# Residual additions of the mixer layers: from VectorE to an identity product on TensorE and bias reads on ScalarE

## The chip, the cores and the metric

The kernel runs on one core of one Trainium2 chip. The metric is the device time of the whole program in microseconds (us): the median over several runs. One execution was also taken with the hardware profiler, and all lines of a profile in this document come from such an execution.

## The reference, cut to what matters

The input is 16 sequences of 512 positions with 128 features, in fp32. Two blocks of the form x = x + s * silu(g) follow each other. In the first block, s comes from a four-layer "mixer" stack and g from a mixture of 8 experts; in the second block, s comes from windowed attention and g from a mixture of 32 experts with one shared expert. Both s and g read the normalised x. The change touches one thing alone, the layers of the first block's mixer stack:

```python
def _layer(x, p):
    ln1w, ln1b, aw, ab, pw, pb, ln2w, ln2b, fw, fb, mw, mb = p
    x = x + _attention(_layernorm(x, ln1w, ln1b), aw, ab, pw, pb)
    h = _layernorm(x, ln2w, ln2b)
    h = jax.nn.gelu(h @ fw + fb, approximate=False) @ mw + mb
    return x + h
for i in range(L):            # L = 4
    x = _layer(x, ...)
```

Here `_attention` is a projection to q, k and v, elementwise quaternion products of the three, a spectral filter over heads and head dimensions, and an output projection `pw` with bias `pb`. So each layer adds its input x twice to a product: once to the attention projection, once to the second MLP product, each time with a bias per feature.

## The kernel before, in words

Features lie on the 128 partitions and positions on the free axis. The program has two phases. The first, up to about 2,900 us, holds the mixer stack and both mixtures of experts. The second, from there to 4,108 us, is the windowed attention of the second block; the change does not touch it.

In the first phase four mixer streams p = 0 to 3 (`mixer_stream`) run side by side. Each takes the eight even or the eight odd sequences, one half of 256 positions each time, and takes every half through four layers (`mixer_layer`). There are 16 sequences x 2 halves x 4 layers = 128 mixer layers in all. Every stream has one PSUM bank of its own, `m0` to `m3`, with a single buffer: each product of a layer takes the bank over from the product before it, once that one has been read. The layer normalisation (`norm`) squares the sequence on ScalarE (line 185), takes the mean by one-column products (L189), adds eps on ScalarE (L198), raises to -0.5 on GpSimd (L200), spreads the result over the partitions by products with the identity (L203), and multiplies on VectorE (L213). The features have been rotated beforehand so that the mean sits in one component and drops out of the variance.

The residual sums are these two statements, one after the projection (`po`, L506) and one after the second MLP product (`pm`, L524):

```python
nc.vector.scalar_tensor_tensor(s1, in0=po, scalar=turned[:, l, 0:1], in1=s, op0=ALU.add, op1=ALU.add)
nc.vector.scalar_tensor_tensor(s2, in0=pm, scalar=turned[:, l, 1:2], in1=s1, op0=ALU.add, op1=ALU.add)
```

They are L508 and L526. Each is followed by a `yield`, and then by a norm of its result: s1 goes to the layer's second norm, s2 to the first norm of the next layer, or out of the stack after the fourth.

The experts share the four engines with the mixers. `loop0` takes one sequence through 8 experts of 256 hidden columns (products L299, L301, L305; Silu L303; multiplication L304), one expert at each of its steps; `loop1` takes one through 16 pairs of experts and the shared one (products L405, L407, L419; Silu L409; multiplications L410 and L418). `prep0` and `prep1` normalise and route. `loop1` of a sequence can start only when both of its mixer halves have written x (`written`), and the mixers of a sequence need what `prep0` and `loop0` leave in `given`.

The order of the work is set in two stages. First, Python generators write the program out: each turn advances every mixer stream by one `yield`, and feeds the experts by a rate, so that `due` steps come due:

```python
STEPS_M, STEPS_0, STEPS_1 = 41, 9, 18
pair = turn // STEPS_M
rate = ((STEPS_0 if pair < 7 else 0) + (STEPS_1 if pair else 0)) / (2 * STEPS_M)
```

41 is the number of yields that a mixer stream takes for one half sequence: ten in each of four layers and one at the end. Second, a scheduler puts the instructions of each engine in a fixed order when the program is built. It prefers those written out earlier, and mixer instructions count as 400 places earlier than they are (`AHEAD`). On the chip each engine then works through its own list in order.

Of the kernel before, what the change touches and what calls it, by code (L numbers as in the profile page):

```python
# [11 lines left out]
AF = mybir.ActivationFunctionType  # L12
ALU = mybir.AluOpType
# [7 lines left out]
L = 4  # L21
# [26 lines left out]
W_QKV, W_PROJ, W_FC, W_MP, W_END = 0, 3, 4, 8, 12  # L48
# [7 lines left out]
def recurrent_kernel(ctx: ExitStack, tc: tile.TileContext, a, out):  # L56
    nc = tc.nc
# [29 lines left out]
    ident = cst[:, C_ID : C_ID + P]  # L87
# [8 lines left out]
    filt = cst[:, C_G : C_G + S]  # L96
# [21 lines left out]
    turned = const.tile([P, L, 2], F32, name="turned")  # L118
# [54 lines left out]
            nc.vector.tensor_copy(w[:, first : first + n, :].rearrange("p j m -> p (j m)"), pt[:, : n * P])  # L173


    def norm(src, dst, sq, bank, name, xs=None, p="e"):


        if xs is not None:
            xc = bank(f"xc_{name}")  # L180
            nc.tensor.matmul(xc, lhsT=centre, rhs=src, start=True, stop=True)
            nc.scalar.activation(sq, xc, AF.Square)
            nc.scalar.copy(xs, xc)
        else:
            nc.scalar.activation(sq, src, AF.Square)
        pv = bank(f"pv_{name}")
        n = src.shape[-1] // P
        for k in range(n):
            nc.tensor.matmul(  # L189
                pv[:, k : k + 1],  # L190
                lhsT=sq[:, k * P : (k + 1) * P],
                rhs=mean_col if xs is not None else mean_col0,
                start=True,
                stop=True,
            )
        yield
        ve = small.tile([P, NBLK], F32, tag=f"ve{p}", name=f"ve_{name}", bufs=2)
        nc.scalar.activation(ve[:, :n], pv[:, :n], AF.Identity, bias=eps)  # L198
        rs = small.tile([P, NBLK], F32, tag=f"rs{p}", name=f"rs_{name}", bufs=2)
        nc.gpsimd.tensor_tensor(rs[:, :n], in0=ve[:, :n], in1=nhalf[:, :n], op=ALU.pow)  # L200
        bc = bank(f"bc_{name}")
        for k in range(n):
            nc.tensor.matmul(  # L203
                bc[:, k * P : (k + 1) * P],
                lhsT=rs[:, k : k + 1].to_broadcast([P, P]),
                rhs=ident,
                start=True,
                stop=True,
            )
        if xs is not None:  # L210
            nc.vector.tensor_mul(dst, bc[:, : n * P], xs)
        else:
            nc.vector.tensor_mul(dst[: P - 1], bc[: P - 1, : n * P], src[: P - 1])  # L213
        yield
# [209 lines left out]
        yield  # L424


    def mixer_layer(l, s, big, A, filt, last, bank, pool, name, p):


        first, last = last  # L430
        w = lw[l]


        qkv = big.rearrange("p (i c) t -> p i c t", c=4)

        sq, h, z = big[:, 1, :], normed[p], big[:, 0, :]
        yield from norm(s, h, sq, bank, f"{name}a", p=p)
        raw, steps, turns = qkv[:, :, 0, :], qkv[:, :, 1, :], qkv[:, :, 3, :]
        for at in (slice(0, 2), slice(2, 3)):
            pq = bank(f"pq{at.start}_{name}")[:, : (at.stop - at.start) * T]  # L440
            for i in range(at.start, at.stop):
                j = (i - at.start) * T
                nc.tensor.matmul(pq[:, j : j + T], lhsT=w[:, W_QKV + i, :], rhs=h, start=True, stop=True)
            pq = pq.rearrange("p (i t) -> p i t", t=T)
            nc.scalar.copy(raw[:, at], pq)

            nc.scalar.activation(turns[:, at], pq, AF.Identity, bias=quarter, scale=1.0 / (2.0 * math.pi))
        for i in range(3):

            nc.sync.dma_start(qkv[8:, i, 2, :], qkv[: P - 8, i, 0, :])  # L450
            nc.sync.dma_start(qkv[:8, i, 2, :], qkv[P - 8 :, i, 0, :])
        for i, n in ((0, 2), (2, 1)):
            at = slice(i, i + n)
            d = (raw[:, at, 1:T], raw[:, at, 0 : T - 1])
            nc.gpsimd.tensor_sub(steps[:, at, 1:T], *(d if i else d[::-1]))
            if not first:
                d = (raw[:, at, 0:1], last[:, at].unsqueeze(2))
                nc.gpsimd.tensor_sub(steps[:, at, 0:1], *(d if i else d[::-1]))
        if first:
            nc.gpsimd.memset(steps[:, :, 0:1], 0.0)  # L460
            nc.gpsimd.tensor_copy(last.unsqueeze(2), raw[:, :, T - 1 : T])
        yield

        n = A[:, 0:3, :]
        nc.vector.tensor_scalar_add(
            n.rearrange("p i (u t) -> p u i t", u=2), turns.rearrange("p i (u t) -> p u i t", u=2), MAGIC
        )
        nc.vector.scalar_tensor_tensor(turns, in0=n, scalar=-MAGIC, in1=turns, op0=ALU.add, op1=ALU.subtract)
        for at, scale in ((slice(0, 3, 2), -TWO_PI_BELOW), (slice(1, 2), TWO_PI_BELOW)):
            nc.scalar.activation(turns[:, at, :], turns[:, at, :], AF.Sin, scale=scale)  # L470
        yield
        q, k, vv = (qkv[:, i, :, :] for i in range(3))

        def rows(x, m):

            x = x.rearrange("p (b a) t -> p a b t", a=2)
            x = x[:, ::-1] if m & 1 else x
            return x[:, :, ::-1] if m & 2 else x


        for m in range(4):
            pr = pool.tile([P, 2, 2, T], F32, tag=f"pr{p}", name=f"pr_{name}{m}", bufs=1)
            nc.vector.tensor_mul(pr, rows(q, 0), rows(k, m))
            first, second = pr[:, 0], pr[:, 1]
            if m == 0:
                nc.vector.tensor_sub(first, first, second)
                nc.vector.tensor_sub(A[:, 0, :], first[:, 0, :], first[:, 1, :])
            elif m == 1:
                nc.vector.tensor_add(first, first, second)
                nc.vector.tensor_add(A[:, 1, :], first[:, 0, :], first[:, 1, :])  # L490
            elif m == 2:
                nc.vector.tensor_sub(first, second, first)
                nc.vector.tensor_add(A[:, 2, :], first[:, 0, :], first[:, 1, :])
            else:
                nc.vector.tensor_add(first, first, second)
                nc.vector.tensor_sub(A[:, 3, :], first[:, 0, :], first[:, 1, :])
        nc.vector.tensor_mul(A, A, vv)
        nc.vector.tensor_add(A[:, 0:2, :], A[:, 0:2, :], A[:, 2:4, :])
        yield

        py = bank(f"py_{name}")[:, :T]
        for i in range(2):
            nc.tensor.matmul(py, lhsT=dht, rhs=A[:, i, :], start=(i == 0), stop=(i == 1))
        nc.vector.tensor_mul(z, py, filt)
        po = bank(f"po_{name}")[:, :T]
        nc.tensor.matmul(po, lhsT=w[:, W_PROJ, :], rhs=z, start=True, stop=True)  # L506
        s1 = pool.tile([P, T], F32, tag=f"s{p}", name=f"s1_{name}", bufs=2)
        nc.vector.scalar_tensor_tensor(  # L508
            s1, in0=po, scalar=turned[:, l, 0:1], in1=s, op0=ALU.add, op1=ALU.add
        )  # L510
        yield
        yield from norm(s1, h, sq, bank, f"{name}b", p=p)
        hid = A
        for i in range(0, 4, 2):
            pf = bank(f"pf{i}_{name}")
            for j in range(2):
                nc.tensor.matmul(
                    pf[:, j * T : (j + 1) * T], lhsT=w[:, W_FC + i + j, :], rhs=h, start=True, stop=True
                )
            nc.scalar.activation(hid[:, i : i + 2, :], pf.rearrange("p (j t) -> p j t", t=T), AF.Gelu)  # L520
        yield
        pm = bank(f"pm_{name}")[:, :T]
        for j in range(4):
            nc.tensor.matmul(pm, lhsT=w[:, W_MP + j, :], rhs=hid[:, j, :], start=(j == 0), stop=(j == 3))  # L524
        s2 = pool.tile([P, T], F32, tag=f"s{p}", name=f"s2_{name}", bufs=2)
        nc.vector.scalar_tensor_tensor(  # L526
            s2, in0=pm, scalar=turned[:, l, 1:2], in1=s1, op0=ALU.add, op1=ALU.add
        )
        yield
        return s2  # L530

    def mixer_stream(seqs, half, pool, bank, p, given, written):

        at = slice(half * T, (half + 1) * T)
        for b in seqs:
            name = f"f{b}h{half}"
            while b not in given:
                yield
            z, _, last = given[b]
            s = z[:, at]  # L540
            for l in range(L):
                big = pool.tile([P, 12, T], F32, tag=f"big{p}", name=f"big_{name}l{l}")
                A = pool.tile([P, 4, T], F32, tag=f"A{p}", name=f"A_{name}l{l}")
                s = yield from mixer_layer(
                    l, s, big, A, filt[:, at], (half == 0, last[:, l, :]), bank, pool, f"{name}l{l}", p
                )
            while given[b][1] is None:
                yield
# [400 lines left out]
```

## Time and profile before

| | us |
|---|---|
| median of 3 runs | 4114.49 |
| lowest and highest | 4114.02, 4125.91 |
| the profiled execution | 4109.77 |
| its span, first to last instruction | 4108.0 |
| busy in the span: TensorE (PE) | 3861.7 |
| VectorE (DVE) | 3461.3 |
| ScalarE (ACT) | 2465.7 |
| GpSimd (POOL) | 1641.1 |

The profile names PE for TensorE's products and PEld for its weight loads, DVE for VectorE, ACT for ScalarE, POOL for GpSimd and SP for the engine that issues most of the transfers. A product of fp32 operands shows as two pairs of weight load and matmul, so the counts of PE are twice the number of calls. "Idle before" is the time in which an engine stood still just ahead of an instruction, and the releaser named after it is what ended that. The view by stretches of time gives each engine's busy time between two moments; the view of waits sums who waited for whom.

### The profile page before, as it was taken

The numbers are of one execution on the slowest core, as the hardware profiler recorded it, in microseconds if no ns is written. First come the engines' busy times: TensorE is split into PE (matmuls) and PEld (weight loads), VectorE is DVE, ScalarE is ACT, GpSimd is POOL, SyncE is SP. The second block draws the span as 40 slices with busy tenths as digits, with TensorE's granted clock in tenths as the row PEclk, the third lists the DMA queues.
The fourth block names the chain that finished last, engine by engine and source line by source line (L and its number), as shares of the span: only waits on it lengthen the run. The fifth ranks groups of instructions, "written<-read, shape, count | busy, mean of one in ns | idle before, by whom it ended". The sixth has DMA issues, their size and how long they took to land. (4 is left out here: it accounts for less than half of the span.)

```text
span 4108.0 us, 56711 instructions
## 1 busy us (share of the span) xinstructions
PE 3861.7 (94%) x16936; PEld 2329.9 (57%) x16936; DVE 3461.3 (84%) x8220; ACT 2465.7 (60%) x5543; POOL 1641.1 (40%) x1885
## 2 busy tenths in 40 slices
PE   8999999998999999999999998879999999999999
PEld 5555666665655656556566555544455555555555
DVE  5788999899889989989988999985677777777776
ACT  3555566655756556556655654633577777777776
POOL 1222322223222232222232223220577777777776
PEclk9999999999999999999999999989999999999999
DMA  3222333323332332442343232424100000000000
GB/s 116 80 82 85 97 90 114 113 73 109 122 91 87 112 112 80 120 120 78 104 122 95 77 114 84 123 66 134 59 11 19 14 19 14 11 19 14 19 4 6
DMA packets 205971, 308.95 MB, mean 75 GB/s; under 512 B 29664, under 2 KB 121952, under 8 KB 205536
## 3 DMA queue, kind: packets, MB, share of 16 engines
q1 hardware_dynamic: 205520, 304.28, 24.9%
q8 instruction: 135, 2.21, 0.2%
q14 instruction: 172, 1.41, 0.1%
q10 hardware_dynamic: 144, 1.05, 0.1%
HBM read 236.79 MB, written 18.09 MB: 62 GB/s over the span
## 5 line engine op out<-in xcount | busy, mean ns | idle before, releaser
L409 ACT ACTIVATE h_m<-pg_m 128x512 f32<-128x512 f32 x272 | 162.2, 596 | 280.5 <-PE pg_m L405 199.3
L405 PE MATMUL pg_m<-xn_m,w_m 128*128 128x512 f32 x544 | 289.3, 614 | 37.6 <-DMA w_m<-in_ew 25.8
L305 PE MATMUL acc_e<-h_e,w_e 128*128 128x512 f32 x512 | 273.8, 617 | 23.9 <-DVE h_e L304 23.6
L419 PE MATMUL acc_m<-h_m,w_m 128*128 128x512 f32 x544 | 284.6, 606 | 8.2 <-DVE h_m L418 8.1
L407 PE MATMUL pu_m<-xn_m,w_m 128*128 128x512 f32 x544 | 287.1, 610 | 5.6 <-DVE h_m L410 5.3
L299 PE MATMUL pg_e<-xn_e,w_e 128*128 128x512 f32 x512 | 268.7, 606 | 12.1 <-ACT h_e L303 10.6
L303 ACT ACTIVATE h_e<-pg_e 128x512 f32<-128x512 f32 x256 | 152.6, 596 | 202.7 <-PE acc_e L305 114.8
L301 PE MATMUL pu_e<-xg_e,w_e 128*128 128x512 f32 x512 | 265.0, 599 | 0.0
L410 DVE TENSOR_TENSOR h_m<-pu_m,h_m 128x512 f32<-128x512 f32 x272 | 185.3, 681 | 73.3 <-PE pu_m L407 63.9
L520 ACT ACT_TABLE_LOAD x187 | 239.9, 1283 | 3.3
L304 DVE TENSOR_TENSOR h_e<-pu_e,h_e 128x512 f32<-128x512 f32 x256 | 174.7, 682 | 70.4 <-PE pu_e L301 67.9
L675 POOL TENSOR_TENSOR t_q<-t_q,rtab 128x512 f32<-128x512 f32 x128 | 162.9, 1273 | 90.5 <-DMA g_a<-g 86.9
L418 DVE TENSOR_TENSOR h_m<-gb_m,h_m 128x512 f32<-128x512 f32 x256 | 182.3, 712 | 14.7 <-DMA gb_m<-gd 13.6
L301 PEld LDWEIGHTS pu_e<-xg_e,w_e 128*128 128x128 f32 x512 | 98.5, 193 | 124.7 <-issue 124.7
L405 PEld LDWEIGHTS pg_m<-xn_m,w_m 128*128 128x128 f32 x544 | 94.9, 192 | 125.9 <-issue 75.8
L676 POOL TENSOR_TENSOR q<-q,t_q 128x512 f32<-128x512 f32 x128 | 163.3, 1276 | 0.1
L675 POOL TENSOR_TENSOR t_k<-t_k,rtab 128x512 f32<-128x512 f32 x128 | 162.9, 1273 | 0.9 <-DVE t_k L673 0.9
L676 POOL TENSOR_TENSOR k<-k,t_k 128x512 f32<-128x512 f32 x128 | 162.8, 1272 | 0.2
L687 PE MATMUL pv<-wv,xn_a 128*128 128x512 f32 x256 | 143.7, 645 | 11.0 <-DVE q L674 10.9
L670 PE MATMUL pa_q<-xn_a,aw 128*128 128x512 f32 x256 | 145.7, 651 | 5.5 <-DMA xn_a<-xn 5.5
L305 PEld LDWEIGHTS acc_e<-h_e,w_e 128*128 128x128 f32 x512 | 90.6, 193 | 96.3 <-DVE h_e L304 47.9
L419 PEld LDWEIGHTS acc_m<-h_m,w_m 128*128 128x128 f32 x544 | 99.8, 193 | 77.1 <-issue 42.7
(6272 smaller groups left out, 11176.4 us busy)
## 6 DMA issues: line engine op xcount, KB each, us to landing
gb_m<-gd SPq DMA_DIRECT2D x512, 128.0 KB
w_m<-in_ew SPq DMA_DIRECT2D x272, 192.0 KB
w_e<-in_ew SPq DMA_DIRECT2D x128, 384.0 KB
gb_e<-gd SPq DMA_DIRECT2D x128, 256.0 KB
x_e<-in_xT SPq DMA_DIRECT2D x16, 256.0 KB
x_m<-x SPq DMA_DIRECT2D x16, 256.0 KB
xn<-xn_m SPq DMA_DIRECT2D x16, 256.0 KB
g<-g_m SPq DMA_DIRECT2D x16, 256.0 KB
```

The costliest lines, as they stand in the source:

```text
L299: nc.tensor.matmul(pg, lhsT=w[:, c, :], rhs=xn, start=True, stop=True)
L301: nc.tensor.matmul(pu, lhsT=w[:, 2 + c, :], rhs=xg, start=True, stop=True)
L304: nc.vector.tensor_mul(h, pu, h)
L305: nc.tensor.matmul(acc, lhsT=w[:, 4 + c, :], rhs=h, start=(e == 0 and c == 0), stop=(e == NE0 - 1 and c == HID0 // P - 1),)
L405: nc.tensor.matmul(pg, lhsT=w[:, 0, :], rhs=xn, start=True, stop=True)
L407: nc.tensor.matmul(pu, lhsT=w[:, 1, :], rhs=xn, start=True, stop=True)
L410: nc.vector.tensor_mul(h, pu, h)
L418: nc.vector.tensor_mul(h, gb, h)
L419: nc.tensor.matmul(acc, lhsT=w[:, 2, :], rhs=h, start=(c == 0), stop=shared)
L520: nc.scalar.activation(hid[:, i : i + 2, :], pf.rearrange("p (j t) -> p j t", t=T), AF.Gelu)
L675: nc.gpsimd.tensor_mul(t, t, rtab[:, 2 * which + 1, :])
L676: nc.gpsimd.tensor_add(dst, dst, t)
```

## The change

The two additions on VectorE are taken out. TensorE starts the sum in PSUM instead: a product of the identity matrix with the sequence (`s` or `s1`) opens the accumulation, and the projection or the four MLP products add to it. `norm` gets the bank and the bias (`summed`) and reads the bank twice on ScalarE: once for the square, once, as Identity with the bias, to write the sequence to SBUF. After the fourth layer there is no norm, and one Identity writes the result. The `yield` that followed the first addition is gone, so that a half sequence takes 37 turns; `STEPS_M` stays 41.

```diff
-    def norm(src, dst, sq, bank, name, xs=None, p="e"):
+    def norm(src, dst, sq, bank, name, xs=None, p="e", summed=None):
...
+        elif summed is not None:
+            nc.scalar.activation(sq, summed[0], AF.Square, bias=summed[1])
+            nc.scalar.activation(src, summed[0], AF.Identity, bias=summed[1])
         else:
             nc.scalar.activation(sq, src, AF.Square)
...
-        yield from norm(s, h, sq, bank, f"{name}a", p=p)
+        yield from norm(s, h, sq, bank, f"{name}a", p=p, summed=summed)
...
-        nc.tensor.matmul(po, lhsT=w[:, W_PROJ, :], rhs=z, start=True, stop=True)
+        nc.tensor.matmul(po, lhsT=ident, rhs=s, start=True, stop=False)
+        nc.tensor.matmul(po, lhsT=w[:, W_PROJ, :], rhs=z, start=False, stop=True)
         s1 = pool.tile([P, T], F32, tag=f"s{p}", name=f"s1_{name}", bufs=2)
-        nc.vector.scalar_tensor_tensor(
-            s1, in0=po, scalar=turned[:, l, 0:1], in1=s, op0=ALU.add, op1=ALU.add
-        )
-        yield
-        yield from norm(s1, h, sq, bank, f"{name}b", p=p)
+        yield from norm(s1, h, sq, bank, f"{name}b", p=p, summed=(po, turned[:, l, 0:1]))
...
+        nc.tensor.matmul(pm, lhsT=ident, rhs=s1, start=True, stop=False)
         for j in range(4):
-            nc.tensor.matmul(pm, lhsT=w[:, W_MP + j, :], rhs=hid[:, j, :], start=(j == 0), stop=(j == 3))
+            nc.tensor.matmul(pm, lhsT=w[:, W_MP + j, :], rhs=hid[:, j, :], start=False, stop=(j == 3))
         s2 = pool.tile([P, T], F32, tag=f"s{p}", name=f"s2_{name}", bufs=2)
-        nc.vector.scalar_tensor_tensor(
-            s2, in0=pm, scalar=turned[:, l, 1:2], in1=s1, op0=ALU.add, op1=ALU.add
-        )
-        yield
-        return s2
+        if l == L - 1:
+            nc.scalar.activation(s2, pm, AF.Identity, bias=turned[:, l, 1:2])
+        yield
+        return s2, (pm, turned[:, l, 1:2])
```

More of the change, by code (lines that the diff above doesn't have):

```diff
@@ L424, in loop1, with mixer_layer @@
         yield
-    def mixer_layer(l, s, big, A, filt, last, bank, pool, name, p):
+    def mixer_layer(l, s, summed, big, A, filt, last, bank, pool, name, p):
         first, last = last
@@ L539, in mixer_stream @@
             z, _, last = given[b]
-            s = z[:, at]
+            s, summed = z[:, at], None
             for l in range(L):
@@ L543, in mixer_stream @@
                 A = pool.tile([P, 4, T], F32, tag=f"A{p}", name=f"A_{name}l{l}")
-                s = yield from mixer_layer(
-                    l, s, big, A, filt[:, at], (half == 0, last[:, l, :]), bank, pool, f"{name}l{l}", p
+                s, summed = yield from mixer_layer(
+                    l, s, summed, big, A, filt[:, at], (half == 0, last[:, l, :]), bank, pool, f"{name}l{l}", p
                 )
```

## The prediction

> **What bounds the kernel now.** I read the page's totals and slices first, then the busy time by stages, then who waits for whom in the long stage, then the order on the engines at one place. The page:
>
> ```profile
> span 4108.0 us, 56711 instructions
> PE 3861.7 (94%) x16936; PEld 2329.9 (57%) x16936; DVE 3461.3 (84%) x8220; ACT 2465.7 (60%) x5543; POOL 1641.1 (40%) x1885
> ...
> PE   8999999998999999999999998879999999999999
> DVE  5788999899889989989988999985677777777776
> ACT  3555566655756556556655654633577777777776
> ```
>
> Up to slice 26 two engines are nearly full at once, TensorE and VectorE. From slice 29 on there is only the second phase, which has none of the changed lines. The mixers end near 2,800 us and the last experts near 2,905 us, so I cut the first phase there:
>
> ```profile
> 300.00:2400.00 2100.00, 1984.99 (x7542) 1250.58 (x7541) 1908.07 (x3474) 1254.02 (x2099) 580.96 (x648) 0.99 0.34 100
> 2400.00:2800.00 400.00, 342.19 (x1268) 222.15 (x1267) 345.87 (x610) 199.76 (x341) 104.01 (x114) 0.92 0.31 89
> 2800.00:2905.00 105.00, 94.90 (x224) 40.64 (x224) 51.92 (x106) 24.46 (x40) 2.29 (x2) 0.93 0.55 170
> ```
>
> The columns are stretch, length, then busy us of PE, PEld, DVE, ACT, POOL. In the long stage PE is busy for 94.5% and DVE for 90.9%: 115 us and 192 us are left. Shares so close don't say who paces whom; the waits do. For DVE and then for PE, in that stage, the longest are:
>
> ```profile
> DVE h_e L304 <- PE pu_e L301: 47.1, 37, 3.5
> DVE h_m L410 <- PE pu_m L407: 17.0, 19, 3.8
> ```
>
> ```profile
> PE pg_m L405 <- DMA w_m<-in_ew: 15.4, 26, 1.6
> PE acc_e L305 <- DVE h_e L304: 11.4, 18, 1.9
> PE pg_e L299 <- ACT h_e L303: 9.5, 11, 2.5
> ```
>
> DVE mostly stands still for TensorE's products. TensorE stands still for a bit of everything, and all its listed waits for DVE come to some 20 us (11.4 here, 4.2 for L410, 1.9 for L418 and small ones). So TensorE leads, by a little. What one call costs it is seen from the starts in a full stretch:
>
> ```profile
> 1505.47 1.02 PE L301 MATMUL pu_e<-xg_e,w_e 128*128 128x512 f32 x2
> 1506.33 1.02 PE L299 MATMUL pg_e<-xn_e,w_e 128*128 128x512 f32 x2
> 1507.19 1.03 PE L517 MATMUL pf_f8h0l<-normed,lw 128*128 128x256 f32 x4
> 1508.05 1.03 PE L517 MATMUL pf_f8h1l<-normed,lw 128*128 128x256 f32 x4
> 1508.92 1.02 PE L299 MATMUL pg_e<-xn_e,w_e 128*128 128x512 f32 x2
> ```
>
> Starts lie 0.86 us apart, for one call of 512 columns (x2) as for two of 256 (x4): a 256-column call takes 0.43 us of TensorE.
>
> **Added on TensorE.** Two identity products of 128x256 per mixer layer, 128 layers: 256 calls x 0.43 = 110 us. Can they hide? The one for `po` needs the stream's bank, which comes free when L504 has read `py`; the old first product waited for L504's result anyway. The one for `pm` needs the bank from the second Gelu (L520), which the old first `pm` product needed too. So neither adds a wait, neither fills an existing hole, and every expert product behind them in TensorE's list starts 0.43 us later. Here a rule of the Trainium skill has to be weighed: "Perfetto Trace Analysis", section "Identifying the Most-Contended Engine", says that matmul busy time is no good measure of TensorE's headroom, and to take the share of weight loads (or the share of peak arithmetic) instead. By PEld, 1250.58 of 2100, there is 40% of room, the 110 us would cost nothing and DVE's relief would decide. But the starts leave no hole between calls, and the 0.86 us would not shrink for a lower PEld share. I count by the starts and charge +110 (ends: +20, if most of the 115 us of idle time can be refilled by another order; +110).
>
> **Removed from VectorE.** L508 and L526, 128 each. Their rows have medians around 0.475 us, for example
>
> ```profile
> L508 DVE SCALAR_TENSOR_TENSOR s_f2h0l<-po_f2h0l,turned,s_f2h0l x3: 475/476/476, 495.4 to 653.8; 128x256 f32<-128x256 f32 x3
> L526 DVE SCALAR_TENSOR_TENSOR s_f2h0l<-pm_f2h0l,turned,s_f2h0l x4: 471/479/484, 426.7 to 675.6; 128x256 f32<-128x256 f32 x4
> ```
>
> 256 x 0.476 = 122 us less on DVE. With TensorE leading, that is worth only what TensorE waits for DVE, about 20 us, and what the new order gains from a freer DVE. I take -20 (ends 0 and -60).
>
> **Added on ScalarE.** 256 Identity reads with a bias (224 in norms, 32 after the last layer), and 224 squares that now take a bias from SBUF and read PSUM. No row shows either; the nearest are a 256-column read of PSUM with a bias, and the square of today:
>
> ```profile
> 1505.73 0.49 ACT L447 ACTIVATE big_f9h1l<-pq_f9h1l,quarter 128x256 f32<-128x256 f32 x1
> ```
>
> ```profile
> L185 ACT ACTIVATE big_f2h0l<-s_f2h0l x7: 407/417/418, 395.9 to 654.4; 128x256 f32<-128x256 f32 x7
> ```
>
> I take L447's 0.49 for both (ends 0.37, the copy L445 without bias, and 0.60): 256 x 0.49 + 224 x 0.07 = 141 us more. The Trainium skill speaks against the move: "ScalarE: Activation LUTs", section "Rules for kernel authors", says to keep additions and multiplications on VectorE. By the rows the two engines cost the same here (0.476 against 0.49, fp32), and ACT is busy for 60% of the stage where DVE is at 91%. The rule would charge more than 141 us to ACT; either way that lies beside TensorE. ACT goes from 60% to about 65%. In its list Identity stands behind the square and waits for nothing new; Silu, Gelu and copies behind it come up to 0.49 us later, and TensorE's listed waits for ACT, about 40 us in the stage, grow a little: +5 (ends 0 and +40). Square, Identity and Copy show no table load at their lines before (loads stand at the lines of Gelu, Silu, Sigmoid and Sin), so I charge none; another mix of Gelu and Silu could move that number, 1.28 us each, either way.
>
> **The norm's chain.** Before: `po`, addition 0.48, square 0.42, then the `pv` products. Now: identity product 0.43, `po`, square 0.49, Identity 0.49 before `pv` may take the bank. That is +0.5 us of work, less one hop over DVE's full list. It has four streams and the experts beside it, so I charge nothing; without that cover it is 64 norms per stream x 0.5 = 32 us, and a table load in front of each read could make it over 100. L200 on POOL waits for the same chain; POOL is at 28%. No transfer is added or moved, and SP's list keeps its content.
>
> **The feed.** The `yield` that goes makes a half sequence 37 turns, while the rate still divides by 41. Up to turn 287 the feed runs as before. The streams now end at turn 8 x 37 + 15 = 311, with 18 + 18 + 246 x 108/82 + 24 x 72/82 = 381 of 432 expert steps written out. Before, 396 were out by turn 328, and the other 36 wait for the last sequences in any case. So 15 expert steps, 3 products of 0.86 us each, 39 us of TensorE work, move from beside the mixers to the end. That suits the end: in 2400:2800 PE stands still for 58 us where the long stage's share would be 22, and in 2800:2905 for 10 more. Of these 46 us I take -30 (ends 0 and -46). The feed also falls behind the mixers: the normalised input of the last sequences comes about 28 turns, some 240 us, later against its need than now. It is ready 300 us ahead today (line 258's last write near 2171, the stream's start near 2473), so no stream should wait.
>
> **Sum** against the profiled execution's 4109.77: +110 - 20 + 5 - 30 = +65, so 4175. The median shown, 4114.49, lies 5 us above that execution, inside the scatter of the three runs.
>
> **The rivals.**
>
> 1. TensorE pays (0.58): 4175, own range 4130 to 4235.
>
> 2. VectorE was the pace-setter (0.20), the other sign. For it: both are above 90%, and the two additions sit in the mixers' chain, which has most of the work of DVE (L483 alone 4 x 1.22 us a layer). Against it: the waits above. Price: from 300 to 2800 DVE is busy for 2254 of 2500 us. At an unchanged share, 112 us less (the part of the 122 that lies in this stretch) would bring 124 us, but PE with 2327 + 104 then meets its own limit; at 98% it needs 2481 us. That is -19, and with the refilled end about -40: 4070. It decides if the new trace shows PE above 97% in the long stage.
>
> 3. It cancels (0.12): refilled idle time and the better end eat the 110 us. 4112.
>
> 4. The longer chain shows (0.10): Square and Identity queue behind Gelu, Silu and their table loads (1.28 + 0.60 us), the bank is held, and all four streams slow down. 64 x (0.5 + 1.9) = 154 us; half of it on top of the first case: 4250. For it: TensorE already waits for ACT at L299 and L405. Against it: ACT has 40% of idle time, and the old square stood in the same list.
>
> That the change does less than it says can be excluded by the code: every addition of both kinds is replaced, in all 128 layers.
>
> **How the numbers follow.** Point: 4175. The range 4065 to 4245 takes in case 2 and 3 and most of case 1's bounds; half of case 4, a little of case 1 above and the best part of case 2 below are left out, some 2 in 10. A measurement of this kernel can tell about 0.3%, 12 us, from no change. Faster: case 2, 0.20. Within: most of case 3 and an edge of case 1, 0.13. Slower: the rest, 0.67. As two signs hold most of the chance, the likeliest case's own range is given above.
>
> **What would show it.** Right: L508 and L526 gone from DVE, its share in the long stage near 85%; 512 more matmuls on PE, at 0.215 us between starts, its share 95 to 96%; ACT near 65%; the mixers' end about where it was, and a longer experts-only stretch behind them. The feed's step is wrong if the stretch from the mixers' end to the second phase is not longer than now or has as much idle PE. The sum is wrong if DVE's waits for TensorE do not grow; it fails altogether if the first phase ends before 2,890 us, or if PE's share falls while its waits for ACT grow, which would be the fourth case.

## The result and the profile after

The changed kernel takes 4136.53 us (median of 6 runs, 4131.11 to 4143.91), the kernel before 4114.26 us (6 runs). The ratio is 1.0054, with a 95% interval of 1.0038 to 1.0069: slower by 22 us, where 65 were forecast. The profiled execution has a span of 4130.8 us, 22.8 more than before.

First the page of the changed kernel, its span, its totals, and the slices of the three engines:

```profile
span 4130.8 us, 58061 instructions
PE 3942.3 (95%) x17448; PEld 2420.7 (59%) x17448; DVE 3386.9 (82%) x7964; ACT 2658.4 (64%) x5865; POOL 1634.6 (40%) x1885
...
PE   8899999999999999999999999989899999999999
DVE  5878889888779989988888788985677777777776
ACT  3566666676666667767655666753576677777776
```

TensorE has the 512 matmuls more (two for each of 256 fp32 products), VectorE the 256 instructions less. VectorE's busy time fell by 74 us (3461.3 to 3386.9) and ScalarE's rose by 193 (2465.7 to 2658.4). The stages, in the same columns as before (stretch, length, busy us of PE, PEld, DVE, ACT, POOL). The three numbers behind POOL are TensorE's mean granted clock, with 1.00 for full speed, the share of the transfer engines, and GB/s. The last stage ends at 2,930 here, since the first phase ends some 23 us later:

```profile
300.00:2400.00 2100.00, 2008.63 (x7793) 1302.32 (x7792) 1828.03 (x3202) 1380.57 (x2309) 564.26 (x641) 0.99 0.32 96
2400.00:2800.00 400.00, 374.10 (x1425) 244.40 (x1425) 348.47 (x629) 249.41 (x418) 108.70 (x116) 0.96 0.34 103
2800.00:2930.00 130.00, 120.00 (x296) 52.78 (x295) 63.80 (x123) 33.41 (x55) 5.13 (x5) 0.99 0.53 166
```

In the long stage PE went from 94.5% to 95.6%, DVE from 90.9% to 87.0%, ACT from 59.7% to 65.7%. From 2400 to 2800 PE stands still for 26 us in place of 58. Most of that comes from two places near the end of the first phase. Here they are in the kernel before and then in the changed one:

```profile
2487.00:2552.00 65.00, 46.74 (x200) 34.09 (x199) 60.11 (x114) 29.42 (x56) 27.41 (x26) 0.90 0.22 65
2750.00:2800.00 50.00, 37.77 (x128) 26.06 (x128) 33.78 (x80) 17.15 (x25) 5.49 (x6) 0.72 0.06 20
```

```profile
2487.00:2552.00 65.00, 61.95 (x246) 39.38 (x244) 57.87 (x91) 43.44 (x76) 25.16 (x22) 1.00 0.41 124
2750.00:2800.00 50.00, 44.14 (x152) 26.82 (x151) 36.54 (x81) 27.70 (x40) 5.87 (x7) 0.90 0.31 96
```

In the kernel before no expert product of L419 ran between 2487 and 2552: the next sequence still had to be prepared. In the changed kernel the experts are 100 us or more further back by then, so there is always one to run.

The granted clock differs too, and the prediction has no term for it. In the first of the two places it is 0.90 before and 1.00 after, in the second 0.72 and 0.90. In these traces it stands at 1.00 or at 0.50; what lies between is a mean. Where it is 0.50, a product takes twice as long. Here are two stretches of the kernel before, one at each clock, and four matmuls of 256 columns that start in each (start, duration):

```profile
2770.00:2775.00 5.00, 5.00 (x16) 4.27 (x16) 0.99 (x2) 1.34 (x3) 0.78 (x1) 0.50 0.00 0
2785.00:2790.00 5.00, 5.00 (x22) 3.52 (x21) 4.58 (x25) 4.66 (x6) 0.00 (x0) 1.00 0.01 2
```

```profile
2770.43 1.91 PE L503 MATMUL py_f15h0l<-A_f15h0l,cst 128*128 128x256 f32 x4
2785.83 1.03 PE L517 MATMUL pf_f15h0l<-normed,lw 128*128 128x256 f32 x4
```

Over the whole trace, the starts of such matmuls lie 0.43 us apart at 0.50 and 0.22 at 1.00 (medians). So the 0.43 us that the prediction charges for a call, which is two matmuls, holds at the full clock alone. Over the whole span the mean granted clock is 0.982 before and 0.989 after. It also varies from run to run: the runs of the kernel before that stand beside the experiments took 4103 to 4114 us where it was 0.983 or more, and 4121 to 4127 where it was 0.978 or less. Whether the time follows the clock there, or both follow something else, no run here separates.

The waits of VectorE in the long stage:

```profile
DVE h_e L307 <- PE pu_e L304: 64.8, 33, 5.6
DVE h_m L413 <- PE pu_m L410: 26.6, 25, 3.7
DVE h_m L413 <- ACT h_m L412: 22.8, 18, 4.8
```

L307 and L413 are L304 and L410 of before. Their waits for TensorE grew from 47.1 and 17.0, as the forecast wanted. The third line is the one to note: before it read `DVE h_m L410 <- ACT h_m L409: 4.7, 5, 1.3`. ScalarE has become a cause of waits, but for VectorE: summed over all lines of the long stage, VectorE's waits for ScalarE went from 37 to 98 us, while TensorE's went from 43 to 25.

The new instructions themselves lasted as long as was charged. One sum, on PE and ACT, as the timeline has it (start, duration):

```profile
1509.87 0.59 PE L509 MATMUL po_f8h0l<-s_f8h0l,cst 128*128 128x256 f32 x2
1510.30 0.59 PE L510 MATMUL po_f8h0l<-big_f8h0l,lw 128*128 128x256 f32 x2
1511.62 0.47 ACT L185 ACTIVATE big_f8h0l<-po_f8h0l,turned 128x256 f32<-128x256 f32 x1
1511.97 0.48 ACT L186 ACTIVATE s_f8h0l<-po_f8h0l,turned 128x256 f32<-128x256 f32 x1
```

The identity product holds TensorE for 0.43 us from start to start, and the two reads take 0.47 and 0.48 us. What ScalarE does beside them did change. The loads of activation tables at the lines of Gelu and of the first experts' Silu, before and then after, where L303 has become L306:

```profile
L520 ACT ACT_TABLE_LOAD x187 | 239.9, 1283 | 3.3
...
L303 ACT ACT_TABLE_LOAD x95 | 121.9, 1283 | 7.0 <-PE pv_m L189 3.3 <-PE pv_e L189 1.3 <-DVE xn_m L211 0.7
```

```profile
L520 ACT ACT_TABLE_LOAD x218 | 279.7, 1283 | 3.8
...
L306 ACT ACT_TABLE_LOAD x116 | 148.8, 1283 | 2.2 <-PE pv_e L192 0.2
```

Counted over all lines, the loads went from 447 to 513, so 66 x 1.28 = 85 us more of ScalarE, because Gelu and Silu alternate more often in the new order.

### The profile page after: what moved, and what is told of

Same layout as the page of the kernel before. It is cut to its first block, busy times and chain, and to the rows that moved or that the text cites. A ratio compares the mean times of both kernels' runs of the same rounds, so it can differ in the third digit from the quotient of the medians.

```text
span 4130.8 us, 58061 instructions
## 1 busy us (share of the span) xinstructions
PE 3942.3 (95%) x17448; PEld 2420.7 (59%) x17448; DVE 3386.9 (82%) x7964; ACT 2658.4 (64%) x5865; POOL 1634.6 (40%) x1885
## 5 line engine op out<-in xcount | busy, mean ns | idle before, releaser
L410 PE MATMUL pu_m<-xn_m,w_m 128*128 128x512 f32 x544 | 284.5, 605 | 8.3 <-DVE h_m L413 8.3
L413 DVE TENSOR_TENSOR h_m<-pu_m,h_m 128x512 f32<-128x512 f32 x272 | 186.1, 684 | 122.2 <-PE pu_m L410 83.5
L304 PE MATMUL pu_e<-xg_e,w_e 128*128 128x512 f32 x512 | 264.0, 597 | 0.0
L306 ACT ACTIVATE h_e<-pg_e 128x512 f32<-128x512 f32 x256 | 152.9, 597 | 171.6 <-PE acc_e L308 83.1
L307 DVE TENSOR_TENSOR h_e<-pu_e,h_e 128x512 f32<-128x512 f32 x256 | 174.7, 682 | 92.7 <-PE pu_e L304 91.1
L304 PEld LDWEIGHTS pu_e<-xg_e,w_e 128*128 128x128 f32 x512 | 98.3, 192 | 123.6 <-issue 123.6
L410 PEld LDWEIGHTS pu_m<-xn_m,w_m 128*128 128x128 f32 x544 | 98.3, 192 | 88.7 <-issue 52.8
```

The lines of the kernel that those rows point to most:

```text
L304: nc.tensor.matmul(pu, lhsT=w[:, 2 + c, :], rhs=xg, start=True, stop=True)
L306: nc.scalar.activation(h, pg, AF.Silu)
L410: nc.tensor.matmul(pu, lhsT=w[:, 1, :], rhs=xn, start=True, stop=True)
L413: nc.vector.tensor_mul(h, pu, h)
```

## The experiments

Two theories stood at the start. The first: VectorE was nearly as much a pace-setter as TensorE, and its relief paid for the products. The second: the feed, which the missing `yield` slows against the mixers, paid most of it back. A third came later: the order that the scheduler makes decides. Each run has its own runs of the kernel before beside it on the same chip (medians 4110 to 4118).

| run | what differs | us | ratio to before, 95% interval |
|---|---|---|---|
| e1 | changed kernel, feed at true pace | 4170.52 | 1.0129 (1.0114 to 1.0145) |
| e2 | before, slower feed (45) | 4193.04 | 1.0175 (1.0153 to 1.0197) |
| e3 | before, products alone | 4193.61 | 1.0185 (1.0171 to 1.0199) |
| e4 | before, additions to ScalarE and GpSimd | 4242.43 | 1.0306 (1.0292 to 1.0320) |
| e5 | changed kernel without the products | 4067.22 | 0.9880 (0.9863 to 0.9896) |
| e6 | e1 without the products | 4137.92 | 1.0048 (1.0035 to 1.0061) |
| e7 | changed kernel, products twice | 4226.26 | 1.0256 (1.0237 to 1.0274) |
| e8 | changed kernel, feed 45 | 4129.99 | 1.0034 (1.0025 to 1.0042) |
| e9 | changed kernel, VectorE's load given back | 4167.73 | 1.0123 (1.0105 to 1.0140) |
| e10 | before, feed 43 | 4178.77 | 1.0152 (1.0135 to 1.0170) |
| e11 | before, mixers' lead 350 | 4134.84 | 1.0049 (1.0036 to 1.0062) |
| e12 | changed kernel, mixers' lead 350 | 4161.09 | 1.0109 (1.0093 to 1.0124) |
| e13 | before, ScalarE's new load alone | 4208.43 | 1.0224 (1.0205 to 1.0243) |
| e14 | before without the yield | 4141.02 | 1.0054 (1.0035 to 1.0073) |
| e15 | the change for `po` alone | 4162.04 | 1.0110 (1.0092 to 1.0129) |
| e16 | the change for `pm` alone | 4123.41 | 1.0018 (1.0008 to 1.0028) |
| e17 | changed kernel with the yield | 4169.34 | 1.0130 (1.0108 to 1.0151) |
| e18 | e16 with feed 45 | 4153.04 | 1.0093 (1.0072 to 1.0113) |

**e1 and e17: the same work at the old pace.** e1 sets the feed's constant to the 37 turns that the change leaves; e17 leaves it at 41 and puts the yield back.

```diff
-STEPS_M, STEPS_0, STEPS_1 = 41, 9, 18
+STEPS_M, STEPS_0, STEPS_1 = 37, 9, 18
```

```diff
+        yield
         yield from norm(s1, h, sq, bank, f"{name}b", p=p, summed=(po, turned[:, l, 0:1]))
```

> The changed kernel with the feed's constant set to the true 37 turns, so that the experts are written out beside the mixers as before. Theory 1 (VectorE was nearly as much a pace-setter as TensorE, and its relief refilled TensorE's idle time): no change, 4136 +- 12. Theory 2 (the slower feed paid most of it back): 15 expert steps of 2.6 us and the idle end come back, so 4165 to 4180, and the end of the mixers moves out by 40 us.

> The changed kernel with the yield put back, between the projection and the norm: 41 turns, a feed of 41, as in the kernel before. If the turns cost what e14 shows and the work cancels: 4110 to 4125. If the slower feed was a gain for the changed kernel, as e1 against it says (34 us): 4160 to 4180.

Measured 4170.52 and 4169.34, as the second theory had it. Two different ways to the old pace agree within 1.2 us, which speaks for a real effect: the work of the change costs 55 to 59 us, and the slower feed that comes with it takes 33 to 34 back. How it does so is less clear, for the two get there differently. The mixers' end, expected 40 us later in e1, is near 2,795 there and near 2,839 in e17 (changed kernel: 2,804), and behind it the experts alone run for 158 us in e1 and 118 in e17 (changed kernel: 114).

**e2, e10: a slower feed without the change.** The constant alone, 45 and 43 in the kernel before.

> The kernel before with nothing but a slower feed: 45 in place of 41, the ratio that the change makes without saying so. Theory 1: 4114 +- 12. Theory 2: the end of the first phase fills up and the kernel gets faster by 30 to 46 us, 4070 to 4085.

> The kernel before with the feed between 41 and 45. If a slower feed harms the kernel before by a mechanism (VectorE sets the mixers' pace there, and work that is moved behind them is only added at the end), half of what 45 did: 4140 to 4165. If 45 was an unlucky order: 4114 +- 15, or scatter without a trend.

77 and 62 us slower. The second theory fails in its simple form: a slower feed is no gain in itself. It helps the changed kernel and harms the old one, and more than either expectation allowed. In e2 the mixers ended near 2,848 us (before: 2,797), and one of the last sequences of experts was stretched over 183 us (2690 to 2873) where it took 73.

**e3: the products alone.** TensorE starts the sums, VectorE reads the bank and adds the bias.

```diff
+        nc.tensor.matmul(po, lhsT=ident, rhs=s, start=True, stop=False)
-        nc.tensor.matmul(po, lhsT=w[:, W_PROJ, :], rhs=z, start=True, stop=True)
+        nc.tensor.matmul(po, lhsT=w[:, W_PROJ, :], rhs=z, start=False, stop=True)
-        nc.vector.scalar_tensor_tensor(s1, in0=po, scalar=turned[:, l, 0:1], in1=s, op0=ALU.add, op1=ALU.add)
+        nc.vector.tensor_scalar_add(s1, po, turned[:, l, 0:1])
```

(the same for `pm` and s2)

> The kernel before with the identity products on TensorE, but VectorE still reads the bank (one addition of the bias instead of the two), so TensorE gets 110 us more and VectorE is hardly relieved; yields and feed as before. Theory 1: TensorE's price shows in full, 4200 to 4225. Theory 2: the price of the products without the feed's help, some 4165 to 4200. If TensorE has hidden room, 4114 to 4130.

78 us slower, in the range of the second theory: 110 us of products on an engine at 94% cost 0.7 of their time.

**e4: the additions off VectorE, without TensorE.**

```diff
-        nc.vector.scalar_tensor_tensor(s1, in0=po, scalar=turned[:, l, 0:1], in1=s, op0=ALU.add, op1=ALU.add)
+        nc.scalar.activation(s1, po, AF.Identity, bias=turned[:, l, 0:1])
+        nc.gpsimd.tensor_add(s1, s1, s)
```

> The kernel before with both additions off VectorE and nothing more on TensorE: ScalarE reads the bank with the bias, GpSimd adds the sequence in SBUF. VectorE loses 122 us, TensorE none. Theory 1: faster by 50 to 100 us, 4015 to 4065. Theory 2: VectorE's relief is worth 0 to 20 us, and the longer chain over GpSimd may cost it, 4095 to 4130.

127 us slower, outside both. It puts ScalarE and then GpSimd into the mixers' chain, so it says less of VectorE than it was meant to; it did raise the question of what ScalarE's load costs.

**e5, e6, e7: the products taken away and doubled.** e5 and e6 leave the two identity products out of the changed kernel and of e1 (the residual additions are then missing from the computation); e7 writes each twice.

```diff
-        nc.tensor.matmul(po, lhsT=ident, rhs=s, start=True, stop=False)
-        nc.tensor.matmul(pm, lhsT=ident, rhs=s1, start=True, stop=False)
```

> The changed kernel without its two identity products per layer (the residual additions are left out of the computation): the relief of VectorE and the reads on ScalarE alone, nothing more on TensorE. Theory 1 (TensorE leads, so its 110 us are paid nearly whole): 4025 to 4050. Theory 2 (VectorE was the other half of the bound and the relief is what pays for the products): also below before, but the products cost only 40 to 70, so 4065 to 4095. Theory 3 (the order that the scheduler makes, with its Gelu and Silu table loads, decides; products and relief matter less): 4100 to 4160.

> The same without the identity products (the residual additions are left out of the computation), and with the feed's constant at the true 37 turns. Against the changed kernel with 37 it gives the products' price a second time: theory 1 4060 to 4085, theory 2 4095 to 4130, theory 3 4130 to 4190. Against before it gives the worth of moving the additions off VectorE at an unchanged feed: my prediction had 0 to 60 us, so 4055 to 4115.

> The changed kernel with each identity product written twice (the second starts the sum anew, so the result is the same): another 110 us of TensorE work at the same places. Theory 1: 4225 to 4250. Theory 2: TensorE is by then the only bound, so also 90 to 110 more. If TensorE still has gaps that fill: 4150 to 4190.

The price of the products is 4136.5 - 4067.2 = 69 us at the slower feed, and 4170.5 - 4137.9 = 33 at the true one; the second set costs 4226.3 - 4136.5 = 90. So it rises as TensorE fills. By their expectations e5 spoke for the second theory, e6 for the third, and e7 for the first two, which both expected 90 us or more. From 300 to 2800 us, first e6 and then e1:

```profile
300.00:2800.00 2500.00, 2320.30 (x8753) 1464.69 (x8751) 2182.35 (x3807) 1636.57 (x2730) 689.71 (x755) 0.98 0.33 99
```

```profile
300.00:2800.00 2500.00, 2370.15 (x9190) 1539.66 (x9189) 2166.14 (x3789) 1663.86 (x2749) 687.89 (x759) 0.99 0.32 97
```

e1 gets 437 more matmuls into the same 2,500 us, and PE is busy for only 50 us more. The traces say where the rest went. The table sums each profiled execution up to its last expert product. Busy time of TensorE in stretches at half clock counts half as work; the other half is the loss by the clock. The ends of matmuls are modelled, so the work is good to some 15 us.

| kernel | first phase | work at full clock | loss by half clock | TensorE idle |
|---|---|---|---|---|
| before | 2895 | 2625 | 54 | 215 |
| changed | 2918 | 2724 | 39 | 156 |
| e6, old pace, no products | 2923 | 2625 | 69 | 229 |
| e1, old pace, with products | 2952 | 2725 | 47 | 180 |
| e5, changed without products | 2853 | 2612 | 51 | 190 |
| e7, changed, products twice | 3009 | 2820 | 40 | 149 |
| e3, before with products | 2978 | 2724 | 53 | 201 |
| e13 (below) | 2997 | 2638 | 77 | 282 |

At the old pace (e6 to e1) the products bring 100 us of work, but TensorE stands still for 49 us less and loses 22 less by the clock. At the slower feed (e5 to the changed kernel) the two are 35 and 12. In e3, where VectorE keeps its load, they are only 14 and 2, and for the second set in e7 7 and nothing. So a good part of the first set's work came back as less idle time and less half clock. That VectorE's relief makes the room for it would fit e3; each row is one order, so it is not shown.

e6 carries a second message. It moves the additions off VectorE with nothing more on TensorE, at the old pace, and is 22 us slower than the kernel before, where 0 to 60 us of gain were expected.

**e8, e11, e12: the order alone.** e8 slows the feed of the changed kernel further; e11 and e12 set the mixers' lead (`AHEAD`) to 350 in the two kernels.

> The changed kernel with a feed slower still, 45 against the true 37. If a slower feed pays because it fills the end of the first phase, that is done (idle PE there is down to 4 us), so 4130 to 4150; if it pays by relieving the mixers' stretch, 4105 to 4125; if the gain from 37 to 41 was luck of the order, anything from 4110 to 4190, with the table loads going along.

> The kernel before with the mixers' lead at 350 in place of 400, which changes the order alone, not the work: how far an arbitrary other order moves it. If the order is a small term: 4100 to 4130. If orders scatter by tens of us, as two runs so far suggest: up to 50 to either side, with the number of table loads going along.

> The same for the changed kernel. If the order is a small term: 4125 to 4150. If not: up to 50 to either side; and then the 22 us between the two kernels as they stand are one draw each from two such scatters.

e8 is 7 us faster than the changed kernel, so most of what the feed can give is given. The lead costs the kernel before 19 us and the changed one 25. A small arbitrary change of order is worth about 20 us, so one difference between two kernels here is no surer than that. Both lie above what a small term would give. At either lead, though, the change costs nearly the same, 22 and 26 us. The number of table loads, which was expected to go along with the time, does not: it is 447 in the kernel before, 507 in e11, 513 in the changed kernel, 487 in the slower e12 and 530 in e5, the fastest.

**e9: VectorE's load given back.** An addition into an unused tile behind each norm.

```diff
+        nc.vector.scalar_tensor_tensor(idle[p], in0=s1, scalar=turned[:, l, 0:1], in1=s1, op0=ALU.add, op1=ALU.add)
```

> The changed kernel with VectorE's relief given back: 256 additions of 128x256 in SBUF behind the norms, into a tile that nobody reads, about 115 us more of VectorE off the mixers' chain. If the relief is what paid for the products (theory 2): 60 to 110 us slower, 4195 to 4245. If TensorE leads and VectorE has room (theory 1): 0 to 20 us, 4136 to 4157.

31 us, between the two expectations, for 97 us more of VectorE's busy time than in the changed kernel (3484.2 against 3386.9). VectorE is no free engine, even at 87%, and no pace-setter either.

**e13: ScalarE's load alone.** The same for ScalarE, in the kernel before.

```diff
+        nc.scalar.activation(idle[p], s1, AF.Identity, bias=turned[:, l, 0:1])
```

> The kernel before with 256 more Identity reads of 128x256 with a bias on ScalarE, behind the norms and into a tile that nobody reads: the change's load on ScalarE alone. If ScalarE's load is the mis-sized term: 25 to 60 us slower, 4140 to 4175, with PE's and DVE's waits for ACT growing. If ScalarE's idle 40% take it, as my prediction said: 0 to 15 us, 4115 to 4130.

90 us slower, beyond both expectations and more than the products cost in e3, on an engine that the page has at 60%. Summed over the first phase of the trace, ACT is busy for 1,751 us in place of 1,625, so 126 more, 20 table loads among them (467 against 447). Its stretch from 300 to 2800 us:

```profile
300.00:2800.00 2500.00, 2287.78 (x8547) 1428.62 (x8546) 2193.78 (x3959) 1531.43 (x2622) 656.00 (x738) 0.98 0.32 97
```

Against 2327.18, 2253.95 and 1453.78 before, ACT does 78 us more here while PE and DVE do 39 and 60 less. Both wait longer for ScalarE: from 300 to 2400 us TensorE's waits for it go from 43 to 64 us, VectorE's from 37 to 70. Two lines of PE's waits from 300 to 2400 us (the first was 9.5 before, the second 7.2 at L405):

```profile
PE pg_e L300 <- ACT h_e L304: 13.9, 13, 3.7
PE pg_m L406 <- ACT h_m L410: 10.2, 10, 2.2
```

In the table above e13 has 67 us more of idle TensorE and 23 more of loss by the clock. It is also a new order, so some 20 us of the 90 may belong to that.

**e14: the yield alone.**

```diff
         nc.vector.scalar_tensor_tensor(s1, in0=po, scalar=turned[:, l, 0:1], in1=s, op0=ALU.add, op1=ALU.add)
-        yield
         yield from norm(s1, h, sq, bank, f"{name}b", p=p)
```

> The kernel before without the yield after the first addition, and nothing else: the same work, 37 turns against a feed of 41. The two runs with a slower feed (43, 45) lost 62 and 77 us on the kernel before; if that is the feed and not the place of the yields: 4165 to 4200. If the missing yield is itself good: 4090 to 4115.

4141.02, between the two expectations: about as slow as the changed kernel, with none of its work. Its feed lags behind the turns by 41 to 37, about as much as 45 to 41 in e2, yet it loses 23 us where e2 loses 77; so the ratio alone does not set the harm. At these turns the move off VectorE brings 4141.0 - 4067.2 = 74 us, and the products take 69 of it.

**e15, e16, e18: halves.** The change for one sum alone: `po` in e15, `pm` in e16, which keeps the yield; e18 is e16 with the feed at 45.

> The change for the first sum alone (po by the identity product, read by ScalarE; pm back on VectorE; the yield gone): 55 us on TensorE, 61 off VectorE. If costs add up: half of the change, 4115 to 4135. If one half holds the cost: 4136 or 4114.

> The change for the second sum alone (pm by the identity product; po on VectorE with its yield, so the feed keeps its true 41 turns). If the true feed costs 34 us as it does in the whole change, 4140 to 4160; if costs add up without that, 4120 to 4140.

> The change for the second sum alone, with the feed at 45 against true 41 turns. If a slower feed pays where VectorE is relieved: 4085 to 4110, faster than both kernels. If half a relief is not enough, it loses like the kernel before: 4150 to 4190.

e15 is 44 us slower, beyond both expectations, and e16 5 to 8, as if costs added up. The halves do not add up to the whole: together 1.3% against 0.5%; they also differ in pace, 37 turns in e15 and 41 in e16. e18 is 43 us slower, so it did not bring a kernel that beats both. Of all runs only e5 is faster than the kernel before, and it leaves the additions out.

## Why the prediction was wrong

**Direction and place.** Slower, in the first phase, with TensorE fuller and VectorE emptier: right. Its signs were met: PE's share 95.6% (95 to 96 forecast), ACT's 65.7% (near 65), DVE's 87.0% (near 85), the mixers' end near 2,804 us (2,797 before), a longer experts-only stretch behind it, 114 us in place of 98, and longer waits of DVE for TensorE. The sum of 65 was three times the 22 measured. That the change is slower does not rest on those 22 alone, which are about what an arbitrary order is worth: it is also slower at the other lead (e12 against e11) and at the old pace (e1, e17).

**The products, +110: the step that failed.** "Neither fills an existing hole, and every expert product behind them in TensorE's list starts 0.43 us later" is right for one place in one order and wrong for the program, since in the new order TensorE stood still less and ran less at half clock. Measured: 33, 69 and 78 us in three settings, and 90 for the second set. The "ends" in the text had room for that (20 to 110), but the value was taken at the upper one. Of some 100 us of work, 49 came back as less idle time and 22 as less loss by the clock at the old pace, 35 and 12 at the pace of the changed kernel. The clock is a term that the prediction did not have. Of the two readings that were weighed, neither holds: TensorE did not have the 40% of room that the share of weight loads gives by the rule in the Trainium skill's "Perfetto Trace Analysis" ("Identifying the Most-Contended Engine"), which would have made the price nothing, nor was the spacing of its starts in a full stretch the price, which would have made it 110.

**The reads on ScalarE, +5: the wrong wait.** Their durations were right; what they cost was read off ACT's idle share and TensorE's waits for ACT. Those waits did not grow but fell, from 43 to 25 us; VectorE's grew, from 37 to 98. "So I charge none" for table loads was wrong too: there are 66 more in the changed kernel, 85 of the 193 us by which ScalarE's busy time grew. What the reads cost in the changed kernel no run isolates. The same load alone cost 90 us in the kernel before (e13), but e5, which leaves only the products out, carries it too and is the fastest of all.

**VectorE's relief, -20.** The 122 us were the sum of durations; over all of VectorE the summed durations fell by 113 and the busy time by 74, since neighbouring instructions overlap. Taken together, relief and reads were -15 in the sum. Measured, the move costs 22 us at the true feed (e6) and brings 74 at the turns of the changed kernel (e5 against e14). Giving VectorE its load back costs 31 (e9). How much of this is the relief and how much the reads stays open.

**The feed, -30.** 34 and 33 measured (e1, e17), so the number was right; the mechanism, a filled end, is shown only in part. After 2400 us, idle TensorE and the loss by the clock come to 70 us in e1, 53 in e17 and 43 in the changed kernel; ahead of it to 157, 183 and 151. Against e1, then, most of the gain lies at the end, against e17 most lies ahead of it. Nor does the slower feed lengthen the stretch of experts alone, which the prediction took as its sign: that is 158 us in e1 and 114 in the changed kernel. That it came out longer than the 98 of the kernel before is luck, as far as the feed goes. And the slower pace harms the kernel before, by 23 (e14), 62 and 77 us. That the old kernel's mixers' stretch lacks the room which the change makes on VectorE would fit; no run separates it from the order, so it stays open.

**The sum as the runs have it:** at the old pace +22 for the move (e6), +33 for the products (e1 less e6), then -34 for the feed (the changed kernel less e1), gives +21. These are steps of one path and so add up by themselves; the path over e14 has +23 (turns), -74 (move) and +69 (products). How a term splits depends on the path, by tens of us, and a single step of 20 to 30 us is hardly more than another order is worth. What holds on both: the products cost well under 110, and the move off VectorE costs at one pace and pays at the other.

**Rivals.** The first, "TensorE pays", is the nearest; its own range of 4130 to 4235 held the time. The second asked for PE above 97% in the long stage, which did not come. The third, which lets refilled idle time eat the 110 us, had part of what the table shows. The fourth asked for longer waits of PE for ACT, and these fell; e13, which leaves the chain as it is, shows that load on ScalarE's list alone can cost time, and no run tries the longer chain by itself.

## What to carry to other kernels

Where three engines work through fixed lists side by side, an engine's share of busy time is not the price of more work on it: here 110 us cost 33 to 90 on the engine at 94%, and 126 us cost 90 on the one at 60%, whose list the other two wait for. Before moving work to a "free" engine, put a dummy of the same load there and measure, and do it under a second setting of the scheduler too, since another order alone was worth 19 and 25 us. Read the granted clock beside the idle time: in the table above it took 39 to 77 us of the first phase. When a change also moves a yield, a rate or a priority, run it once with the pace restored; that part was worth 34 us here, more than the whole difference.

## What was not expected of the hardware

Two reads of one PSUM bank one behind the other on ScalarE start 0.35 us apart in the lines above (1511.62 and 1511.97; median of the 224 pairs 0.37) though each lasts 0.47: they overlap. So 256 Identity reads, charged at 0.49 each, hold the engine for less than their summed durations. Yet such a load alone cost 90 us in e13, as much as the second set of products in e7.
